# Idle PSUM banks lent to two stages in the last turns and to one in the first, with new ranks for the order of the work

## The chip, the cores and the metric

The kernel runs on one core of a Trainium2 chip. The time is the device time of one execution in microseconds (us); less is better. The core has engines that each work through a queue of their own in a fixed order: TensorE (PE) multiplies matrices and transposes, VectorE (DVE), ScalarE (ACT) and GpSimd (POOL) work element by element, and SyncE (SP) issues the DMAs of this kernel. They wait for one another through semaphores. PE writes its results to PSUM, which this kernel divides into eight tiles of 128 partitions by 512 fp32 values, here called banks; ACT and DVE read them from there.

## What is computed

The input `x` has 128 sequences of 64 tokens with 256 features (8,192 tokens), and there is one condition vector of 256 features per sequence. There are two layers, each with a residual sum:

```
x = x + ffn0(scan(cond, x))          # a gated recurrence over the 64 tokens, then an int8-quantized gated feed-forward
x = x + fp6_linear(block(x, cond))   # a hyperbolic transformer block, then a linear layer quantized to fp6
```

`block` works on vectors of a Poincare ball. It takes the log map, a layer norm, a shift and scale from the condition, and attention with 16 heads of 16 features over the 64 tokens of a sequence; then a Moebius addition of the residual; then norm, shift and scale again and a feed-forward part, which the kernel has folded into one 256 x 512 product per token (one half gives the value, the other the norm); then a second Moebius addition. `fp6_linear` scales blocks of 32 features by their largest magnitude, rounds them to a 6-bit grid, and multiplies them by a 256 x 256 weight that is rounded in the same way.

## The kernel before

The first layer's recurrence runs first, then the two products of its feed-forward part. Everything behind that, from about 373 us on, is one fused part (`fused`). It works on 64 tiles of 128 tokens, four tiles to a group (`GT` = 4), so 16 groups (`NGR`). Within a group most things are done for a pair of tiles (`h2`).

A group passes through these stages:

- `front` (matmuls at L908): the last product of the first layer, into bank `dn`;
- `norms` (L1167 on): the layer-norm coefficients, shift and scale, and the clip to the ball (L638 on DVE, L640 on POOL);
- `attention`: transposes (L95) into `qk`, ACT copies the high part (L938), DVE subtracts for the low part (L940), PE makes q, k and v (L950, `qk`), scores (L1007, `sc`), exponentials on ACT (L1016), the product with v (L1026, `ao`), ACT copies it to `raw` (L1030), DVE divides (L1033, L1034), then the output projection (L1059, `ao`) and its scaling on DVE (L1064);
- `tail`: the coefficients of the Moebius sums for a whole group (L774 to L814, with a power on POOL, L651) and the sums (L818);
- `mlp`, the feed-forward: for each pair transposes into `ml`, ACT copy (L1084) and DVE residue (L1086), then for each of the two tiles seven matmuls into `ml` (L1091, L1095), a DVE dot product (L1099) and an ACT copy (L1103) that empty the bank; after the group the scaling (L1110), the gate on POOL (L756) and square sums on ACT (L629);
- `fp6`: block maxima (L1126 to L1132), scaling on POOL (L1134), rounding on ACT (L1138), DVE dequantization (L1142), transposes into `fp`, ACT copy to the tile `yT` (L1151), products into `fp` (L1156, L1158), the residual sum on DVE (L1163), and a DMA to the output.

A loop over turns `k` from -5 to 18 staggers them. In turn `k` group `k` passes `tail`, `norms` and `mlp`, group `k + 5` passes `attention` (`LA` = 5), group `k + 6` passes `front`, and group `k - 3` passes the second half of `tail` and `fp6` (`LM` = 3). So turns -5 to -1 hold no feed-forward, no fp6 before turn 3, no `front` after turn 9, and from turn 11 there is no attention.

The turns are not run one after the other. Every operation gets a priority from its turn and from a table of ranks, and the framework's scheduler, which works while the kernel is built, puts each engine's instructions in order by these priorities and by when it expects data and buffers to be ready:

```
def step(name):
    tc.cur_priority = base + (turn_[0] + LA) * TURN + RANK[name]
```

`TURN` is 1800, so a rank of -5000 lets a stage compete with work of nearly three turns before. The order is then fixed: each engine runs its queue in that order and waits where data is late.

Banks come from pools by name. Their numbers are in `CFG`: `dn` 1, `qk` 2, `sc` 2, `ao` 1, `ml` 1, `fp` 1, eight in all. A pool with one bank makes a stage take turns with its readers: the next use may start only when the engines that read the last use have ended. The tile `yT` of fp6 has one buffer as well, and the output tile `ot` has two.

```
def bank(tag):
    return ps.tile([P, 512], F32, name=tag, tag=tag, bufs=CFG[tag])
```

Of the kernel before, what the change touches and what calls it, by code (L numbers as in the profile page):

```python
# [22 lines left out]
P = 128  # L23
# [19 lines left out]
NG = NT // GN  # L43
AR = 8
TS = 4
CFG = {'rnd': 'S', 'ef': 8, 'fill': {'x1a': 'V', 'mod0': 'V'}, 'hold': [3, 0], 'mk': 2, 'raw': 1, 'mv': 6, 'xs': 3, 'la': 3, 'sb': 7, 'qks': 'GGGG', 'deq': 'VV', 'first': 1000, 'hb': 2, 'q_h': 'P', 'q_x1': 'P', 'q_xr': 'P', 'q_ot': 'P', 'q_out': 'P', 'q_ada': 'P', 'room': [[0.3, 0.3, 0.55], [0.5, 0.4, 0.2]], 'qv': 64, 'p1': 'GVGVGVGV', 'x1': 3, 'u1': 16, 'u2': 6, 'qkv': 2, 'sq': 1, 'uT1': 2, 'uT2': 2, 'qM': 2, 'kT': 2, 'e': 4, 'oT': 1, 'yT': 1, 'hq': 2, 'hl': 2, 'xr': 1, 'ot': 2, 'ada00': 2, 'ada02': 2, 'ada10': 2, 'ada12': 4, 'dn': 1, 'qk': 2, 'sc': 2, 'ao': 1, 'ml': 1, 'fp': 1, 'mod0': 'GGGV', 'mod1': 'VVVV', 'sqm0': 'SSSS', 'sqm1': 'SSSS', 'su0': 'VVVV', 'su1': 'VGVG', 'q8': 'GGGGGG', 'hqc': 'SSSVVV', 'qm': 'SSSS', 'x1a': 'GV', 'gate0': 'GGGG', 'gate1': 'GGGG', 'yb': 'GG', 'va': 'GGGG', 'sqt': 'SSSS', 'sqg': 'SSSS', 'sqo': 'SSVS', 'f2e': 'SSSS', 'early': 0, 'q8f': 'VVVVVV', 'hqf': 'SSSVVV', 'fl': 1, 'un': 2, 'jsu': 1, 'LA': 5, 'LM': 3, 'tl': 6, 'ord': 1, 'xt': 3, 'q_xt': 'P'}
GT = 4
NGR = NTILE // GT

TURN = 1800  # L50
RANK = {"front.q8": 910, "front.cast": 539, "front.mm": -718, "front.x1": -1305, "front.add": 174, "store.x1": 0, "a.turn": -1220, "a.hi": -1577, "a.lo": 495, "a.qkv": 46, "a.qkvcopy": -917, "a.sq": 2253, "a.nh": -44, "chain.h": -8170, "a.qk": -90, "a.va": -90, "a.turnq": -90, "a.qm": -1178, "a.kt": -1474, "a.sc": -90, "a.e": -877, "a.av": -90, "a.raw": -1338, "a.o": 3284, "a.turno": 1011, "a.ot": -3468, "a.wo": 975, "a.proj": -2819, "m.turn": 987, "m.hi": -123, "m.lo": -2161, "m.mm": 1726, "m.dot": -468, "m.copy": 301, "m.a": -355, "f.max": -10889, "f.q": 4682, "f.rnd": -1889, "f.deq": 4033, "f.turn": 167, "f.yt": 4664, "f.mm": 507, "load.ot": 10015, "f.add": -588, "store.out": -58, "x2n": 2724, "own": 641, "load.xt": -636, "chain.su": 4117, "chain.full": -5861, "chain.cf": -1389, "chain.ln": -2069, "chain.tail": -2513, "stats1": 1067, "stats2": 339, "load.mod0": -1252, "load.mod1": -208, "mod0.0": -3294, "mod0.1": -93, "mod0.2": 398, "mod0.3": -712, "mod1.0": 1137, "mod1.1": 2275, "mod1.2": -5509, "mod1.3": 1054, "sqm0": 2326, "sqm1": -1277, "clip0": -1974, "clip1": -1974, "sqt0": 462, "sqt1": -162, "gate0": -1900, "gate1": 755, "sqg0": -808, "sqg1": 4262, "xdot.a": -1630, "xdot.m": 1293, "load.h": -5461, "load.x": 0, "a.sqo": 76, "load.gate0": 3865, "load.gate1": 3539, "comb.a": 708, "comb.m": -2849}

LA, LM = CFG["LA"], CFG["LM"]

# [19 lines left out]
def tile_kernel(ctx, tc, a, out):  # L74
# [70 lines left out]
    with ExitStack() as l0:  # L145
# [15 lines left out]
        with ExitStack() as sc_:  # L161
# [270 lines left out]
            for n in range(T // TS):  # L432
# [5 lines left out]
                for i in range(TS):  # L438
# [22 lines left out]
                    with tc.issue_after(lv.ins), tc.issue_after(ls.ins), tc.issue_after(lp.ins):  # L461
# [4 lines left out]
                        for q in range(2):  # L466
                            if t < CFG["hold"][q]:
                                continue
                            left[q] = [min(l, 0.0) + r for l, r in zip(left[q], CFG["room"][q])]
                            while min(left[q]) > 0:  # L470
# [25 lines left out]
        for b0 in range(0, B, NBB):  # L496
            for c in range(2):

                q8 = xp.tile([P, NBB, T], I8, name="q8", tag="q8")
                src = hsT[:, c, :, b0 : b0 + NBB].rearrange("p t b -> p b t")  # L500
                if b0 < CFG["qv"]:
                    V.tensor_scalar(q8, src, isx, None, ALU.mult)
# [16 lines left out]
        def h_chunk(pg, pu, j, at, dst):  # L519
# [3 lines left out]
            cnt[0] += 1  # L523
            if CFG["p1"][cnt[0] % 8] == "G":
                uv = fw.tile([P, GN], F32, name="uv", tag="uv")
# [34 lines left out]
        V.tensor_scalar(sdh, sd_bc, sh[:, 0:1], None, ALU.mult)  # L560

    fused(ctx, tc, a, out_tok, x_tok, locals())


def fused(ctx, tc, a, out_tok, x_tok, L):
    nc = tc.nc
    V, S, G_, PE = nc.vector, nc.scalar, nc.gpsimd, nc.tensor
# [20 lines left out]
    def move(key, out, in_):  # L588
        Q[CFG["q_" + key]].dma_start(out=out, in_=in_)

    at = [0]
    turn_ = [-LA]
    base = tc.cur_priority + 4000

    def step(name):

        tc.cur_priority = base + (turn_[0] + LA) * TURN + RANK[name]

# [13 lines left out]
    def pick(key, g):  # L612
# [3 lines left out]
            es = CFG["fill"].get(key, es)  # L616
        return es[g % len(es)]

    def bank(tag):
        return ps.tile([P, 512], F32, name=tag, tag=tag, bufs=CFG[tag])  # L620

    def big(tag, shape, dt=F32):
# [253 lines left out]
    def front(i):  # L876
# [4 lines left out]
        for h2 in pairs:  # L881
# [20 lines left out]
            move("xr", out=xr, in_=x_tok[:, i0 + 2 * h2 : i0 + 2 * h2 + 2, :])  # L902
            step("front.mm")
            py = bank("dn")

            for i, j in [(i, j) for i in range(2) for j in range(5)] + [(0, 5), (1, 5)]:
# [12 lines left out]
    def attention(i, u, sums):  # L919
# [4 lines left out]
        for h2 in pairs:  # L924
# [4 lines left out]
            uT = big("uT1", [P, 2, 2, 2 * P], F32R)  # L929
            step("a.turn")  # L930
            pt = bank("qk")
            for c in range(2):
                po = pt[:, c * 256 : (c + 1) * 256].rearrange("p (s g t) -> p s g t", s=2, g=2)
# [7 lines left out]
            for xy in range(2):  # L941
                cs = slice(xy * P, (xy + 1) * P)
                for lo, hi in ((0, 512), (512, 768)):
                    step("a.qkv")
                    pm = bank("qk")
                    n_ = hi - lo
                    PE.matmul(pm[:, :n_], lhsT=ones3[:, lo // 512, :], rhs=rows3[:, :n_], start=True, stop=False)
                    for k in range(2):
                        for q, (w, z) in enumerate(PASSES):
                            PE.matmul(pm[:, :n_], lhsT=uT[:, z, k, cs], rhs=wqkv[:, w, k, lo:hi],  # L950
                                      start=False, stop=(k == 1 and q == 2))
                    step("a.qkvcopy")
                    S.copy(qkv[:, xy, lo:hi], pm[:, :n_])
                step("a.sq")
                sq = big("sq", [P, 3 * D])
                S.activation(sq, qkv[:, xy, :], AF.Square)
                step("a.nh")
                V.tensor_reduce(nh[:, xy * 48 : (xy + 1) * 48], sq.rearrange("p (h d) -> p h d", d=HD),
                                AX.X, ALU.add)
# [342 lines left out]
```

## Time and profile before

| what | value |
|---|---|
| time, median of 3 runs | 1328.8 us (1326.1 to 1334.34) |
| profiled execution: time, span of its records | 1332.73 us, 1331.0 us |
| mean granted TensorE clock | 0.881 |
| PE busy | 1075.1 us (81%) |
| DVE busy | 1128.2 us (85%) |
| ACT busy | 847.8 us (64%) |
| POOL busy | 840.2 us (63%) |
| DVE busy between 378 and 1331 us | 842.0 of 953 us |
| last projection of the last attention (L1064) ends | 1199.7 us |

The busy shares are means over stages with different limits, so they are read stage by stage. An engine that is idle before an instruction has that idle time put down to the instruction that ended last of those it waited for. The chain of work that ended last gives DVE 6% of the span as a share of its own, PE 3%, POOL 3%, DMA 2% and ACT 1%, spread over many lines.

### The profile page before, as it was taken

The page shows a single profiled execution, that of the slowest core. Times are in us where ns is not written, and L with a number is a line of the kernel's source. Part 1 is how long each engine was busy: PE and PEld are TensorE (multiplying, and loading weights), DVE is VectorE, ACT ScalarE, POOL GpSimd, SP SyncE. Part 2 cuts the span into 40 slices and gives each one's busy share as a digit, 9 for nine tenths or more (in the row PEclk, how much of TensorE's full clock was granted, in tenths as well). Part 3 has the DMA queues.
Part 4 walks back from the last instruction along what each step waited for, and adds up shares of the span by engine and source line. Part 5 has one row for each costly group of instructions (what it writes and reads, how often), then busy time and mean ns, then how long its engine had stood idle before and what let it go on. Part 6 is the DMA issues. An engine that isn't in the chain of part 4 may idle for free. (4 is left out here: it accounts for less than half of the span.)

```text
span 1331.0 us, 23828 instructions
## 1 busy us (share of the span) xinstructions
PE 1075.1 (81%) x7382; PEld 742.9 (56%) x7404; DVE 1128.2 (85%) x3337; ACT 847.8 (64%) x2607; POOL 840.2 (63%) x1024
## 2 busy tenths in 40 slices
PE   6999977984479798988889788897888988874756
PEld 5766642332356565655666566675666756653534
DVE  5766769995787779899999999999989999799674
ACT  2455547981467677678667776776778867764331
POOL 3110118864787858878968778776686776764541
PEclk9999979995699899899899899998999869986765
DMA  7721105678843314334335245323432223323211
GB/s 240 294 70 59 54 1 201 262 276 255 259 130 106 126 33 143 113 103 146 113 124 155 89 127 159 96 69 120 135 105 80 65 72 96 96 84 91 80 43 52
DMA packets 119304, 163.64 MB, mean 123 GB/s; under 512 B 10885, under 2 KB 72074, under 8 KB 119178
## 3 DMA queue, kind: packets, MB, share of 16 engines
q1 hardware_dynamic: 119178, 162.13, 38.5%
q8 instruction: 58, 0.95, 0.3%
q14 instruction: 68, 0.56, 0.1%
HBM read 115.94 MB, written 46.14 MB: 122 GB/s over the span
## 5 line engine op out<-in xcount | busy, mean ns | idle before, releaser
L629 ACT ACTIVATE junk<-u 128x256 bf16<-128x256 f32 x432 | 182.2, 425 | 102.8 <-POOL u L756 31.4
L950 PE MATMUL qk<-wqkv,uT 128*128 128x512 f32 (+1 forms) x768 | 180.2, 374 | 10.7 <-ACT uT L938 10.5
L756 POOL TENSOR_TENSOR u<-u,ada 128x256 f32<-128x256 f32 x128 | 100.0, 785 | 86.4 <-ACT junk L629 76.3
L950 PEld LDWEIGHTS qk<-wqkv,uT 128*128 128x128 f32 x768 | 126.1, 202 | 46.5 <-issue 17.6
L1007 PE MATMUL sc<-qM,kT 64*64 64x256 f32 x1024 | 126.7, 412 | 10.9 <-ACT kT L996 9.4
L1095 PE MATMUL ml<-wm,uT 128*128 128x512 f32 (+1 forms) x384 | 122.5, 458 | 0.0
L1095 PEld LDWEIGHTS ml<-wm,uT 128*128 128x128 f32 x384 | 84.7, 223 | 51.0 <-issue 14.7
L1026 PE MATMUL ao<-va,e 128*64 128x34 f32 x2048 | 89.5, 240 | 22.0 <-DVE u L1064 13.1
L1026 PEld LDWEIGHTS ao<-va,e 128*64 128x64 f32 x2048 | 78.7, 154 | 50.1 <-DVE u L1064 16.0
L636 ACT ACTIVATE qM<-sc,mhead 128x256 f32<-128x256 f32 x256 | 102.3, 494 | 5.4 <-PE sc L95 5.4
L908 PE MATMUL dn<-wdT,hq 128*128 128x256 bf16 (+1 forms) x384 | 65.1, 310 | 38.6 <-DVE x L911 17.0
L982 POOL TENSOR_TENSOR va<-qkv,comb 64x256 f32<-64x256 f32 x128 | 87.8, 703 | 5.2 <-PE ao L1026 2.7
L629 ACT ACTIVATION_READ_ACCUMULATOR junk<-u 128x1 f32 x432 | 86.8, 201 | 0.0
L977 POOL TENSOR_TENSOR qkv<-qkv,comb 128x512 f32<-128x512 f32 x64 | 72.9, 1157 | 21.2 <-DVE comb L968 17.2
L1007 PEld LDWEIGHTS sc<-qM,kT 64*64 64x64 f32 x1024 | 56.7, 139 | 51.1 <-ACT kT L996 13.8
L445 PE MATMUL pg<-hsT,WT 128*128 128x128 f32 x504 | 76.4, 293 | 8.2 <-ACT hsT L457 7.9
L640 POOL TENSOR_SCALAR hb<-hl,cu 128x1280 int8<-128x1280 f32 (+1 forms) x64 | 64.5, 1013 | 29.1 <-DMA hl<-h_d 11.1
L1158 PE MATMUL fp<-wfT,yT 128*128 128x256 f32 x256 | 81.6, 450 | 0.0
L445 PEld LDWEIGHTS pg<-hsT,WT 128*128 128x128 f32 x504 | 66.1, 195 | 26.6 <-ACT hsT L457 23.4
L1016 ACT ACTIVATE e<-sc 128x512 f32<-128x512 f32 x128 | 74.7, 603 | 7.3 <-PE sc L1007 3.9
L527 POOL TENSOR_TENSOR hv<-uv,sil 128x512 f32<-128x512 f32 x44 | 57.9, 1318 | 29.7 <-ACT sil L521 13.0
L457 ACT ACTIVATE hsT<-gate 128x128 f32<-128x128 f32 x128 | 39.6, 309 | 53.8 <-DVE gate L456 53.8
(287 smaller groups left out, 3176.5 us busy)
## 6 DMA issues: line engine op xcount, KB each, us to landing
ada<-ada_d SPq DMA_DIRECT2D x128, 256.0 KB, 3.6
h_d<-hv SPq DMA_DIRECT2D x80, 256.0 KB, 2.2
hl<-h_d SPq DMA_DIRECT2D x32, 640.0 KB, 4.7
ada<-ada_d SPq DMA_DIRECT2D x128, 128.0 KB, 2.5
xt<-in_xT_dram SPq DMA_DIRECT2D x16, 512.0 KB, 3.7
xr<-in_x_dram SPq DMA_DIRECT2D x32, 256.0 KB, 4.1
x_d<-x SPq DMA_DIRECT2D x32, 256.0 KB, 2.9
xt<-x_d SPq DMA_DIRECT2D x32, 256.0 KB, 3.0
```

The lines of the kernel that those rows point to most:

```text
L445: lp = PE.matmul(pg[c][:, st], lhsT=WT[:, k, c * P : (c + 1) * P], rhs=hp[:, k, :], start=False, stop=False, skip_group_check=True)
L629: S.activation(junk, src, AF.Square, accum_out=acc)
L636: S.activation(dst, src, AF.Copy, scale=by)
L756: ENG[pick(f"gate{which}", g)].tensor_tensor(av, av, gb, ALU.mult)
L950: PE.matmul(pm[:, :n_], lhsT=uT[:, z, k, cs], rhs=wqkv[:, w, k, lo:hi], start=False, stop=(k == 1 and q == 2))
L977: ENG[pick("qks", g)].tensor_tensor(qk, qk, bc_in(comb[:, xy * 48 : xy * 48 + 32], HD), ALU.mult)
L982: ENG[pick("va", g)].tensor_tensor(va[r, :, s, 0:HD], qkv[r, xy, 512:768].rearrange("p (h d) -> p h d", d=HD), bc_in(comb[r, xy * 48 + 32 ...
L1007: PE.matmul(sc[rr][s * T : (s + 1) * T, c * 256 : (c + 1) * 256].rearrange("p (v t) -> p v t", v=4), lhsT=kTs[xy][r, c, s * T : (s + 1) * ...
L1016: S.activation(e.rearrange("p c v t -> p (c v t)"), sc[rr], AF.Exp, scale=1.0 / math.sqrt(HD))
L1026: PE.matmul(pv[xy * T : (xy + 1) * T, hh], lhsT=E[2 * xy + hh // 4][:, c, hh % 4, :], rhs=vas[(2 * h2 + xy) % 4][:, c * 8 + hh], start=Tru ...
L1095: PE.matmul(pm[:, cs], lhsT=uT[:, z, k, i * P : (i + 1) * P], rhs=wm[:, w, k, cs], start=False, stop=(k == 1 and q == 2))
L1158: PE.matmul(o, lhsT=yT[:, 2 * i + c, :], rhs=wfT[:, c, :], start=False, stop=(c == 1))
```

## The change

The bank of a tile is no longer fixed by its name. In turns -5 to -2 the banks of `attention` that were `ao` alternate between `ao` and `fp`. From turn 11 on the tiles of `mlp` go round `ml`, `qk`, `qk`: three tiles are taken for each pair, first the transposes, then one for each tile's products, so transposes get `ml` and products the two banks of `qk`. From turn 11 on the tiles of `fp6` alternate between `fp` and `dn`, and from turn 15 on they go round `fp`, `dn`, `ao`. Besides, 53 of the 84 ranks have new values; `CFG` has the same values, only one entry stands at another place. No operation is added or taken away, and no shape, type or engine is changed.

```
-RANK = {"front.q8": 910, ... "front.mm": -718, "front.x1": -1305, ... "a.turn": -1220, "a.hi": -1577, ... "a.qm": -1178, ... "a.proj": -2819, ... "m.hi": -123, ... "m.mm": 1726, "m.dot": -468, ... "f.add": -588, "store.out": -58, ... "chain.su": 4117, ... "chain.cf": -1389, ... "load.h": -5461, ... "comb.a": 708, ...}
+RANK = {"front.q8": 582, ... "front.mm": -1046, "front.x1": -1633, ... "a.turn": -405, "a.hi": -6857, ... "a.qm": 1669, ... "a.proj": -7498, ... "m.hi": -1065, ... "m.mm": 1399, "m.dot": -1470, ... "f.add": -4529, "store.out": 2514, ... "chain.su": 2733, ... "chain.cf": 1681, ... "load.h": -8071, ... "comb.a": 4044, ...}
...
+    used = {}
+
     def bank(tag):
+
+        k, tags = turn_[0], (tag,)
+        if tag == "ao" and k < LM - 4:
+            tags = ("ao", "fp")
+        if k >= NGR - LA:
+            tags = {"ml": ("ml", "qk", "qk"), "fp": ("fp", "dn") if k < NGR - 1 else ("fp", "dn", "ao")}.get(tag, tags)
+        n = used[tag] = used.get(tag, -1) + 1
+        tag = tags[n % len(tags)]
         return ps.tile([P, 512], F32, name=tag, tag=tag, bufs=CFG[tag])
```

More of the change, by code (lines that the diff above doesn't have):

```diff
@@ L45 @@
 TS = 4
-CFG = {'rnd': 'S', 'ef': 8, 'fill': {'x1a': 'V', 'mod0': 'V'}, 'hold': [3, 0], 'mk': 2, 'raw': 1, 'mv': 6, 'xs': 3, 'la': 3, 'sb': 7, 'qks': 'GGGG', 'deq': 'VV', 'first': 1000, 'hb': 2, 'q_h': 'P', 'q_x1': 'P', 'q_xr': 'P', 'q_ot': 'P', 'q_out': 'P', 'q_ada': 'P', 'room': [[0.3, 0.3, 0.55], [0.5, 0.4, 0.2]], 'qv': 64, 'p1': 'GVGVGVGV', 'x1': 3, 'u1': 16, 'u2': 6, 'qkv': 2, 'sq': 1, 'uT1': 2, 'uT2': 2, 'qM': 2, 'kT': 2, 'e': 4, 'oT': 1, 'yT': 1, 'hq': 2, 'hl': 2, 'xr': 1, 'ot': 2, 'ada00': 2, 'ada02': 2, 'ada10': 2, 'ada12': 4, 'dn': 1, 'qk': 2, 'sc': 2, 'ao': 1, 'ml': 1, 'fp': 1, 'mod0': 'GGGV', 'mod1': 'VVVV', 'sqm0': 'SSSS', 'sqm1': 'SSSS', 'su0': 'VVVV', 'su1': 'VGVG', 'q8': 'GGGGGG', 'hqc': 'SSSVVV', 'qm': 'SSSS', 'x1a': 'GV', 'gate0': 'GGGG', 'gate1': 'GGGG', 'yb': 'GG', 'va': 'GGGG', 'sqt': 'SSSS', 'sqg': 'SSSS', 'sqo': 'SSVS', 'f2e': 'SSSS', 'early': 0, 'q8f': 'VVVVVV', 'hqf': 'SSSVVV', 'fl': 1, 'un': 2, 'jsu': 1, 'LA': 5, 'LM': 3, 'tl': 6, 'ord': 1, 'xt': 3, 'q_xt': 'P'}
+CFG = {'rnd': 'S', 'ef': 8, 'hold': [3, 0], 'mk': 2, 'raw': 1, 'mv': 6, 'xs': 3, 'la': 3, 'sb': 7, 'qks': 'GGGG', 'deq': 'VV', 'first': 1000, 'hb': 2, 'q_h': 'P', 'q_x1': 'P', 'q_xr': 'P', 'q_ot': 'P', 'q_out': 'P', 'q_ada': 'P', 'room': [[0.3, 0.3, 0.55], [0.5, 0.4, 0.2]], 'qv': 64, 'p1': 'GVGVGVGV', 'x1': 3, 'u1': 16, 'u2': 6, 'qkv': 2, 'sq': 1, 'uT1': 2, 'uT2': 2, 'qM': 2, 'kT': 2, 'e': 4, 'oT': 1, 'yT': 1, 'hq': 2, 'hl': 2, 'xr': 1, 'ot': 2, 'ada00': 2, 'ada02': 2, 'ada10': 2, 'ada12': 4, 'dn': 1, 'qk': 2, 'sc': 2, 'ao': 1, 'ml': 1, 'fp': 1, 'mod0': 'GGGV', 'mod1': 'VVVV', 'sqm0': 'SSSS', 'sqm1': 'SSSS', 'su0': 'VVVV', 'su1': 'VGVG', 'q8': 'GGGGGG', 'hqc': 'SSSVVV', 'qm': 'SSSS', 'x1a': 'GV', 'gate0': 'GGGG', 'gate1': 'GGGG', 'yb': 'GG', 'va': 'GGGG', 'sqt': 'SSSS', 'sqg': 'SSSS', 'sqo': 'SSVS', 'f2e': 'SSSS', 'early': 0, 'q8f': 'VVVVVV', 'hqf': 'SSSVVV', 'fl': 1, 'un': 2, 'jsu': 1, 'LA': 5, 'LM': 3, 'tl': 6, 'ord': 1, 'xt': 3, 'q_xt': 'P', 'fill': {'x1a': 'V', 'mod0': 'V'}}
 GT = 4
@@ L50 @@
 TURN = 1800
-RANK = {"front.q8": 910, "front.cast": 539, "front.mm": -718, "front.x1": -1305, "front.add": 174, "store.x1": 0, "a.turn": -1220, "a.hi": -1577, "a.lo": 495, "a.qkv": 46, "a.qkvcopy": -917, "a.sq": 2253, "a.nh": -44, "chain.h": -8170, "a.qk": -90, "a.va": -90, "a.turnq": -90, "a.qm": -1178, "a.kt": -1474, "a.sc": -90, "a.e": -877, "a.av": -90, "a.raw": -1338, "a.o": 3284, "a.turno": 1011, "a.ot": -3468, "a.wo": 975, "a.proj": -2819, "m.turn": 987, "m.hi": -123, "m.lo": -2161, "m.mm": 1726, "m.dot": -468, "m.copy": 301, "m.a": -355, "f.max": -10889, "f.q": 4682, "f.rnd": -1889, "f.deq": 4033, "f.turn": 167, "f.yt": 4664, "f.mm": 507, "load.ot": 10015, "f.add": -588, "store.out": -58, "x2n": 2724, "own": 641, "load.xt": -636, "chain.su": 4117, "chain.full": -5861, "chain.cf": -1389, "chain.ln": -2069, "chain.tail": -2513, "stats1": 1067, "stats2": 339, "load.mod0": -1252, "load.mod1": -208, "mod0.0": -3294, "mod0.1": -93, "mod0.2": 398, "mod0.3": -712, "mod1.0": 1137, "mod1.1": 2275, "mod1.2": -5509, "mod1.3": 1054, "sqm0": 2326, "sqm1": -1277, "clip0": -1974, "clip1": -1974, "sqt0": 462, "sqt1": -162, "gate0": -1900, "gate1": 755, "sqg0": -808, "sqg1": 4262, "xdot.a": -1630, "xdot.m": 1293, "load.h": -5461, "load.x": 0, "a.sqo": 76, "load.gate0": 3865, "load.gate1": 3539, "comb.a": 708, "comb.m": -2849}
@@ new lines @@
+RANK = {"front.q8": 582, "front.cast": 801, "front.mm": -1046, "front.x1": -1633, "front.add": 166, "store.x1": 0, "a.turn": -405, "a.hi": -6857, "a.lo": 522, "a.qkv": 53, "a.qkvcopy": -1222, "a.sq": 2388, "a.nh": -231, "chain.h": -8170, "a.qk": -90, "a.va": -90, "a.turnq": -90, "a.qm": 1669, "a.kt": -1474, "a.sc": -90, "a.e": -31, "a.av": -90, "a.raw": -1338, "a.o": 3284, "a.turno": 1011, "a.ot": -3468, "a.wo": 975, "a.proj": -7498, "m.turn": 987, "m.hi": -1065, "m.lo": -2129, "m.mm": 1399, "m.dot": -1470, "m.copy": 301, "m.a": -410, "f.max": -10913, "f.q": 4922, "f.rnd": -1889, "f.deq": 4033, "f.turn": 167, "f.yt": 4664, "f.mm": 633, "load.ot": 9947, "f.add": -4529, "store.out": 2514, "x2n": 2132, "own": 385, "load.xt": -406, "chain.su": 2733, "chain.full": -6047, "chain.cf": 1681, "chain.ln": -2762, "chain.tail": -2988, "stats1": 1067, "stats2": -1543, "load.mod0": -1349, "load.mod1": -1335, "mod0.0": -3294, "mod0.1": -225, "mod0.2": 25, "mod0.3": -829, "mod1.0": 1309, "mod1.1": 2275, "mod1.2": -5547, "mod1.3": 1054, "sqm0": 2326, "sqm1": -1277, "clip0": -1974, "clip1": -1974, "sqt0": 368, "sqt1": 30, "gate0": -1937, "gate1": 2179, "sqg0": 523, "sqg1": 4899, "xdot.a": -1758, "xdot.m": 1090, "load.h": -8071, "load.x": 0, "a.sqo": 76, "load.gate0": 1795, "load.gate1": 3539, "comb.a": 4044, "comb.m": -2849}
```

## The prediction

> **What bounds the kernel now.** I read the busy slices first, to find which engine fills which stage. The slices of the page, 40 of 33.3 us, each digit tenths of busy time:
>
> ```profile
> PE   6999977984479798988889788897888988874756
> ...
> DVE  5766769995787779899999999999989999799674
> ...
> PEclk9999979995699899899899899998999869986765
> ```
>
> VectorE (DVE) is at nine tenths or more through most of the second half and falls only in the last five slices, where the granted TensorE clock falls too. The same by stretches, whose borders I put at the ends of single attentions (columns: window, its length, then busy time and count of PE, PEld, DVE, ACT, POOL, clock, DMA share, GB/s):
>
> ```profile
> 378.00:452.00 74.00, 63.14 (x477) 43.16 (x478) 60.45 (x130) 50.10 (x140) 61.20 (x75) 0.90 0.35 109
> 452.00:490.00 38.00, 35.59 (x301) 24.76 (x300) 26.77 (x94) 29.04 (x88) 23.41 (x26) 0.88 0.23 77
> ...
> 811.00:1118.00 307.00, 265.34 (x2162) 196.92 (x2165) 289.72 (x894) 228.21 (x749) 225.76 (x282) 0.91 0.32 97
> 1118.00:1199.00 81.00, 63.60 (x562) 48.84 (x560) 70.46 (x250) 56.40 (x202) 56.98 (x75) 0.94 0.30 94
> 1199.00:1256.00 57.00, 32.44 (x123) 24.37 (x123) 46.39 (x179) 24.52 (x87) 32.54 (x36) 0.71 0.32 97
> 1256.00:1331.00 75.00, 44.44 (x127) 30.30 (x126) 42.69 (x160) 19.89 (x67) 23.10 (x24) 0.55 0.13 42
> ```
>
> Window minus DVE busy is what better order could win: 13.6 + 11.2 us at the entry, 17.3 us in the 307 us middle, 10.6 us in 1199 to 1256 and 32.3 us in the last 75 us. The middle is DVE-bound; banks can't help there, since DVE's work is the same. The place for the new banks is the end, so I read DVE's waits from 1256 us on (us in all, times, longest):
>
> ```profile
> DVE ot L1163 <- PE fp L1158: 15.4, 5, 5.9
> DVE junk L1099 <- PE ml L1095: 5.6, 4, 2.0
> DVE satc L779 <- POOL r L651: 3.8, 2, 2.4
> ```
>
> 21 us of the 32 are waits for the two stages whose banks change. The PE timeline shows why (start, length, work, idle before it and its releaser):
>
> ```profile
> 1259.53 1.12 PE L95 MATMUL ml<-ident,u 128*128 128x128 f32 x4 [0.93 <-ACT u L1103]
> 1262.04 0.59 PE L1091 MATMUL ml<-rows,ones 128*128 128x512 bf16 x1 [1.40 <-DVE uT L1086]
> ...
> 1265.80 0.59 PE L1091 MATMUL ml<-rows,ones 128*128 128x512 bf16 x1 [0.93 <-ACT u L1103]
> ...
> 1269.56 1.11 PE L95 MATMUL ml<-ident,u 128*128 128x128 f32 x4 [0.93 <-ACT u L1103]
> ...
> 1289.58 1.03 PE L1158 MATMUL fp<-wfT,yT 128*128 128x256 f32 x4
> ...
> 1314.51 1.11 PE L95 MATMUL fp<-ident,u 128*128 128x128 f32 x4 [0.79 <-DVE ot L1163]
> ...
> 1321.13 1.12 PE L95 MATMUL fp<-ident,u 128*128 128x128 f32 x4 [0.78 <-DVE ot L1163]
> ```
>
> The last feed-forward tile pair's transpose (1259.53) waits for the copy that empties `ml`, though its input was ready at 1256.6 (L638 ends). The fp6 transpose at 1321.13 waits until DVE has added the pair before it, though its input was ready at 1311.7.
>
> **The change, part by part.**
>
> *Feed-forward, turns 11 to 15.* `ml` then serves transposes alone and the two `qk` banks take the products. From 1256.6 the last turn has two transposes (1.1 us each) and four groups of products (2.83 us each: one of L1091, six of L1095, 1262.04 to 1264.87); a group now starts 3.76 us after the one before it, the two transposes 10 us apart. New: transpose, 0.6 us copy (L1084), 0.7 us residue (L1086), so the first group starts near 1260; the four groups and the other transpose take 4 x 2.83 + 1.1 = 12.4, so the last dot (L1099) ends near 1273 where it ended at 1280.8. DVE's own work up to that dot, summed in the new order with the old rows, is 14.8 us from L638 on, so 1271.4 is its floor. The next step (L1110) has 22.1 us of DVE work from L638 before its end in both orders (1285.3 in the trace), floor 1278.7. From 1285.3 I take 5.5 us off; bounds 0 (DVE or POOL arrives no earlier) and 6.6 (the floor).
>
> *fp6, last turns.* `fp`, `dn` and, from turn 15, `ao` take turns. The last four pairs run 6.62 us apart at the end (1314.51 to 1321.13). Gone from a pair: its transpose behind the add (1.1 + 0.8 us). What stays serial is `yT`, which has one buffer (`yT`: 1): copy 0.6 and products 4.0 (1322.98 to 1326.98), with the gaps 4.7 a pair. Two pairs, from the first of the last two dequantizations (1311.0), would end near 1322.1, not 1327.7: 5.6 us. But the new DVE order puts the add of the pair before (`ot` of turn 17, L1163) in front of the last two dequantizations (L1142). That is a new wait: behind it stand both L1142, and PE's last transposes wait for them. That add needs products that now end near 1312.2 (transposes 1301.3 to 1303.5, products to 1307.5, copy, products), so dequantization ends near 1314.3 and the last add at 1325.2: gain 2.5. The products took 1.03 us a half pair at 1289.58 and 1.91 elsewhere in this stretch, where the granted clock was 1.00 and 0.50; with the second pair of turn 17 and the two behind it at the faster rate the same steps end near 1318.7, a gain of 9. I take 4, nearer the slow rows, since five of the last six pairs ran slow. The output path: loads of `ot` have two buffers and follow on SP the store of two pairs before; store and load took 2.1 + 2.6 us, so behind the add that ends near 1312.9 the last load lands near 1317.6, before its add.
>
> *Earlier drain turns.* The 2.9 us wait of L1099 for PE in 1199 to 1256 is the only other DVE wait on these banks: 1.5 us off, between 0 and 2.9.
>
> *The first turns.* Attentions 0 to 3 alternate `ao` with the idle `fp`. What PE now waits for the emptying of `ao`, from 373 to 550 us:
>
> ```profile
> PE ao L1026 <- ACT raw L1030: 0.5, 1, 0.5
> ```
>
> So the bank costs 0.5 us directly. Behind it DVE waits 6.5 us for `raw` (L1033 <- ACT raw L1030, 378 to 582), mostly latency of the attention itself. I take 1 us, between 0 and 7.
>
> *The new ranks.* 53 of 84 change, so order changes on every engine; no instruction is added or removed, on the DMA queues neither. I weigh it by work: with the old row durations summed along both built orders, when the eighth attention (7) writes its projection (L1064), DVE has done 606 us in the new order and 671 in the old. That looks like a delay of feed-forward, but compare at equal DVE work: in the old order DVE had done 607 us when attention 6 ended, and there PE had 289 us of work behind it and ACT 514; the new order has 293 and 521 at its 606. The engines are as balanced as before; at 514 and 566 us PE and ACT are 12 to 19 us further ahead than before, which is the risk. At the end L638 of the last turn has 1093.9 us of DVE work in front of it, against 1093.4. So I put the ranks at 0, bounds -21 (half of the 42 us of idle of entry and middle) and +32 (below).
>
> *Sum.* 5.5 + 4 + 1.5 + 1 = 12 us. The profiled execution took 1332.7 us for a span of 1331.0, so 1320.7 for its like. It lay 3.9 us over the median of the three runs, 1328.8; from that median the forecast is 1316.8, **1317 us**.
>
> **A rule weighed against it.** The one warm half pair at 1289.58 came after 5 us of nearly unbroken matmuls (1281.57 to 1287.3). The Trainium skill, TensorE: Matmul & The Clock Gate, section "A second HAM failure mode: psum-queue depth-cycling", speaks against a change like this: cycling through banks with short pauses between groups made the clock swing between half and full, and the throughput suffered. By that rule the last products stay slow and the fp6 term is 2.5, the sum 10.5; the same page's Part 1, where some 3.4 us of sustained work frees the clock, would make it 9, the sum 17. No row of this trace shows either with these banks.
>
> **Rivals.**
>
> *Slower: attention runs ahead and DVE starves.* One mechanism, at 450 to 750 us: with less feed-forward work in front of attention 7, DVE has 65 us less filler (671 - 606) while attention's own chain (raw, exponentials, square sums) keeps its length. Against: equal balance above; for: entry stretches, where attention ran with little filler, idle 11.2 of 38 us. If half of the 65 us is lost the run ends at 1317 + 32 = 1349. It decides from 12 us of added idle: attention 7 would have to end later than about 763 us (751 + 12).
>
> *The banks are hidden.* DVE and POOL order, not PE, ends the drain: POOL's power (L651, 2.9 us each) and the ACT/POOL ping-pong of the gates stay. Then only the fp6 lower bound of 2.5 and the earlier turns' 1.5 remain: 4 us, 1325.
>
> *More than forecast.* Denser PE gets its clock in the last 75 us (9 instead of 4, 6.6 instead of 5.5) and the ranks win some 12 of those 42 us: 1317 - 18 = 1299.
>
> *It doesn't do what it says.* The product tile could land on the bank that it waits for anyway; but in the built order the last turns' products sit on `qk` and their transposes on `ml`, so I give this nothing of its own.
>
> **How the numbers follow.** Forecast (1308 to 1323) 0.44, of which 0.22 below 1315.5; more 0.20; hidden (1323 to 1334) 0.16; starving 0.20, of which 0.17 over 1342. This measurement can tell about 1% (13 us) from no change. Faster 0.22 + 0.20 = 0.42; slower 0.17; the same 0.22 + 0.16 + 0.03 = 0.41. The range leaves out the worst of the starving case (0.14) and the best of "more" (0.05): 1298 to 1340.
>
> **What would show it.** L1163's wait for PE after 1256 falls from 15.4 to under 10 us; L1099's falls below 3; the last two fp6 adds stand under 5 us apart where they stood 6.6; PE clock in the last 75 us over 0.55. DVE idle from 378 to 811 stays near 40 us; if it passes 55, the ranks cost what the banks won. The forecast is wrong if L638 of the last turn comes much later or earlier than the same work in front of it says, or if attention 7 ends after 763 us.

## The result: less time at the end, more in the middle

The changed kernel took 1334.43 us in the median of 20 runs (1327.44 to 1341.1), the kernel before 1327.21 us (1320.03 to 1334.34, also 20). The ratio is 1.0051 with a 95% interval of 1.0032 to 1.0071: some 7 us slower, where 12 us faster was forecast. The profiled execution of the changed kernel took 1335.15 us for a span of 1333.4, against 1332.73 and 1331.0 before. So the profile of before lies 5.5 us over its kernel's median and that of the changed kernel 0.7 us, and differences between the two profiles have to be read with that in mind.

Line numbers from L626 on are higher by 10 in the changed kernel (L638 becomes L648, L1163 becomes L1173). The busy slices of its page:

```profile
PE   6999976984579898999887798879989789983754
...
DVE  5766779996687779897898977999979989889876
...
PEclk9999979995589899798987898979989799767978
```

The DVE row shows both halves of the story. The last five slices are fuller in all (89876 where 99674 stood), and the middle has sevens and eights where it had nines. The granted TensorE clock of the last two slices is 7 and 8 where it was 6 and 5.

Windows that end at single attentions say how much. The stretch from the end of attention 3 (its last L1064 or L1074) to the end of attention 13 holds 513 us of DVE work by the old row durations in both kernels. First the kernel before (window, length, then busy time of PE, PEld, DVE, ACT, POOL, clock, DMA share, GB/s):

```profile
582.00:1118.00 536.00, 461.13 (x3715) 341.20 (x3717) 511.65 (x1571) 395.47 (x1290) 408.37 (x497) 0.92 0.36 107
```

and the changed kernel, in its middle and in its last stretch:

```profile
563.00:1125.00 562.00, 487.61 (x3722) 357.79 (x3724) 506.27 (x1559) 399.67 (x1291) 413.94 (x506) 0.89 0.35 106
```

```profile
1266.00:1333.00 67.00, 35.00 (x133) 24.86 (x132) 47.35 (x176) 23.05 (x80) 29.78 (x30) 0.79 0.20 62
```

The same work takes 562 us instead of 536, and DVE is idle for 562 - 506.3 = 55.7 us of it, where it was idle for 24.4. In the last 67 us it is idle for 19.7, where it was for 32.3 in the last 75.

The waits of DVE from 1256 us on answer to those shown of before:

```profile
DVE satc L789 <- POOL r L661: 7.3, 3, 4.6
DVE ot L1173 <- PE dn L1168: 3.1, 1, 3.1
DVE ot L1173 <- PE fp L1168: 2.1, 1, 2.1
...
DVE ot L1173 <- PE ao L1168: 0.6, 1, 0.6
```

The residual add of fp6 waits 5.8 us for PE in all, where it waited 15.4, and the wait of the feed-forward's dot product (5.6 us before) is not in the answer any more. In its place POOL's power (L661) has come forward. On PE the last two turns of fp6 now look like this:

```profile
1314.20 1.08 PE L95 MATMUL dn<-ident,u 128*128 128x128 f32 x4
...
1315.29 1.91 PE L1168 MATMUL fp<-wfT,yT 128*128 128x256 f32 x4
...
1319.52 1.13 PE L1168 MATMUL ao<-wfT,yT 128*128 128x256 f32 x4 [0.73 <-ACT yT L1161]
...
1323.70 0.63 PE L95 MATMUL ao<-ident,u 128*128 128x128 f32 x4
...
1325.54 1.03 PE L1168 MATMUL dn<-wfT,yT 128*128 128x256 f32 x4
```

The second pair's transpose runs beside the first pair's work without a wait, half a pair's products take 1.03 us instead of 1.91 from the second pair on, and the one gap left inside a turn is that for the single tile `yT` (0.73 us).

From the last L638 (L648) to the last residual add, both with as good as the same DVE work in front of them (1093.4 and 1093.9 us), it took 1256.6 to 1327.7 = 71.1 us before and 1276.6 to 1330.1 = 53.5 us after: 17.6 us less. Not all of that is due to the banks: the granted clock differed too, and the run with fp6's banks alone (below) shows that it does so without any change. But that L648 ended 20.0 us later. Where these 20 us arose is seen by subtracting, at the end of single attentions, the DVE work in front (old row durations, summed along the built order) from the time. (That sum comes to 1141 us in all, where DVE was busy for 1128.2 us, so the remainder is somewhat less than DVE's idle time, in all kernels alike. Its differences are what counts.)

| end of attention | 3 | 7 | 8 | 11 | 13 | 15 | last L638/L648 |
|---|---|---|---|---|---|---|---|
| before: time - DVE work, us | 133.5 | 140.7 | 147.5 | 154.4 | 156.2 | 160.7 | 163.2 |
| after | 131.5 | 151.4 | 168.4 | 175.0 | 179.8 | 181.8 | 182.7 |

Up to attention 3, in the turns with the lent bank, nothing is lost. From there to attention 8 the changed kernel loses 23 us (36.9 us of added idle against 14.0), and behind it no more.

What ended DVE's idle time in that middle, before (582 to 1118 us; the answer's largest groups):

```profile
DVE tftc L786 <- ACT zztc L785: 4.3, 4, 2.6
DVE u L739 <- DMA ada<-ada_d: 3.9, 3, 2.6
DVE lnaln L710 <- POOL lnaln L651: 3.8, 4, 1.5
```

and after (563 to 1125 us):

```profile
DVE nh L968 <- ACT sq L966: 6.0, 5, 2.2
DVE uT L950 <- ACT uT L948: 4.8, 3, 2.4
DVE u L749 <- DMA ada<-ada_d: 4.2, 6, 0.9
DVE q L784 <- ACT junk L639: 4.1, 1, 4.1
DVE rden L1043 <- ACT raw L1040: 3.9, 4, 1.4
```

All groups of the two answers summed: 29 waits of 19.6 us before, of which ACT ended 6.8 and PE 0.9; 54 waits of 51.1 us after, of which ACT ended 30.0 and PE 6.4. No single wait stands out. DVE meets, at many places, an instruction whose input is not finished, most often by ACT, and everything behind it in DVE's queue stands still, for 0.9 us in the mean and 4.1 us at most. Three of these instructions belong to attention itself (L968, L950 and L1043): they waited 14.7 us for ACT, where the same three waited 0.6 us before.

### The profile page after: what moved, and what is told of

The parts are those of the page before. It is cut to its first block, busy times and chain, and to the rows that moved or that the text cites. A ratio compares the mean times of both kernels' runs of the same rounds, so it can differ in the third digit from the quotient of the medians.

```text
span 1333.4 us, 23814 instructions
## 1 busy us (share of the span) xinstructions
PE 1092.0 (82%) x7378; PEld 753.7 (57%) x7404; DVE 1117.2 (84%) x3337; ACT 849.4 (64%) x2607; POOL 835.2 (63%) x1024
## 4 chain that ended last, share of the span: by engine, by line
DVE 44%; PE 23%; POOL 11%; ACT 8%; DMA 7%; issue 5%; SPq 0%; POOLq 0%; DVEq 0%; ACTq 0%
PE pg L445 5%; DMA ada<-ada_d 5%; DVE u L828 4%; PE pg L426 3%; DVE u L749 3%; DVE am L530 2%; DVE nh L968 2%; PE sc L1017 2%; PE qk L960 2%; DVE junk L774 2%; DVE hv L529 2%; ACT qM L646 2%; DVE bn L726 2%; POOL r L661 2%; DVE u L648 2%
## 5 line engine op out<-in xcount | busy, mean ns | idle before, releaser
L960 PEld LDWEIGHTS qk<-wqkv,uT 128*128 128x128 f32 x768 | 125.6, 202 | 48.4 <-issue 24.4
L1017 PE MATMUL sc<-qM,kT 64*64 64x256 f32 x1024 | 135.9, 437 | 15.1 <-ACT kT L1006 8.9
L918 PE MATMUL dn<-wdT,hq 128*128 128x256 bf16 (+1 forms) x384 | 69.3, 328 | 38.6 <-DVE x L921 17.7
L1017 PEld LDWEIGHTS sc<-qM,kT 64*64 64x64 f32 x1024 | 59.7, 147 | 59.3 <-issue 17.3
L992 POOL TENSOR_TENSOR va<-qkv,comb 64x256 f32<-64x256 f32 x128 | 84.2, 677 | 10.5 <-PE ao L1036 6.0
L987 POOL TENSOR_TENSOR qkv<-qkv,comb 128x512 f32<-128x512 f32 x64 | 70.6, 1111 | 20.6 <-DVE comb L978 10.0
L1105 PE MATMUL ml<-wm,uT 128*128 128x384 f32 (+1 forms) x264 | 76.7, 424 | 0.0
L968 DVE TENSOR_REDUCE nh<-sq 128x48 f32<-128x768 f32 x64 | 60.1, 939 | 19.4 <-ACT sq L966 19.2
L918 PEld LDWEIGHTS <-hq 128*128 128x128 bf16 (+1 forms) x384 | 38.9, 113 | 65.6 <-ACT junk L639 20.5
```

Source lines behind the costliest of these rows:

```text
L918: PE.matmul(py[:, i * D : (i + 1) * D], lhsT=hq[r, j, i * P : (i + 1) * P], rhs=wdT[r, j, :], start=(i == 0 and j == 0), stop=(j == 5), sk ...
L992: ENG[pick("va", g)].tensor_tensor(va[r, :, s, 0:HD], qkv[r, xy, 512:768].rearrange("p (h d) -> p h d", d=HD), bc_in(comb[r, xy * 48 + 32 ...
L1017: PE.matmul(sc[rr][s * T : (s + 1) * T, c * 256 : (c + 1) * 256].rearrange("p (v t) -> p v t", v=4), lhsT=kTs[xy][r, c, s * T : (s + 1) * ...
L1105: PE.matmul(pm[:, cs], lhsT=uT[:, z, k, i * P : (i + 1) * P], rhs=wm[:, w, k, cs], start=False, stop=(k == 1 and q == 2))
```

## The experiments

Three theories went into the first four kernels. A: the new ranks cost the middle. B: the bank lent in the first turns costs it. C: the end only looks shorter because work was moved out of it.

**The banks of the last turns alone.**

```
-RANK = {new values}
+RANK = {values of before}
...
-        if tag == "ao" and k < LM - 4:
-            tags = ("ao", "fp")
```

> Only the lending of banks from turn 11 on, with the old ranks and no lending in the first turns. Each engine's order is that of the kernel before up to 847 us of DVE work, about 1000 us into the span. In the changed kernel the stretch from the last turn's L638 to the last add shrank from 71 to about 54 us. Theory A (new ranks cost the middle, end banks win the end): 15 to 18 us faster, ratio 0.986 to 0.989. Theory B (the bank lent in the first turns costs the middle): the same ratio, 0.986 to 0.989. Theory C (the end only looks shorter because other work was moved out of it): ratio 0.995 to 1.000.

Measured: ratio 1.0002 (0.9976 to 1.0029). None of the theories had the overall time. The profile again shows a shorter end: from the last L638 to the last add 1274.4 to 1325.2 = 50.8 us, against 71.1, with 4.7 us more DVE work in front of that L638 (1098.1 us against 1093.4). But time less DVE work, which followed the kernel before within 2 to 5 us as far as attention 12 (160.8 against 156.8), had grown to 169.1 at attention 13, 177.4 at 14 and 176.3 at L638, against 156.2, 164.8 and 163.2. The order changed at 847 us of DVE work, about 1000 us into the span, when the new banks changed what the scheduler found ready. So what the end gained was lost again just before it.

**The banks of the last turns with the new ranks, without the one in the first turns.**

```
-        if tag == "ao" and k < LM - 4:
-            tags = ("ao", "fp")
```

> The lending from turn 11 on with the new ranks, without the bank lent to attention in the first turns. Theory A (new ranks cost some 22 us before the end): about as the changed kernel, ratio 1.003 to 1.007. Theory B (the first turns' bank costs it): 15 us faster than before, ratio 0.986 to 0.992.

Measured: 1.0229 (1.019 to 1.0269), far over what either theory gave. Time less DVE work was 155.4 us at attention 7, 181.8 at 11 and 195.9 at 15.

**All lent banks with the old ranks.**

```
-RANK = {new values}
+RANK = {values of before}
```

> All banks lent as in the changed kernel, old ranks. Attention 7 ends with 629 us of DVE work in front of it (671 before, 606 in the changed kernel). Theory A: the loss goes with the ranks, ratio 0.985 to 0.990. Theory B: the loss stays, ratio 1.002 to 1.008.

Measured: 1.0268 (1.0222 to 1.0314). The loss did not go with the ranks as A had it, nor did it stay as B had it: it grew.

**The new ranks alone.**

```
-RANK = {values of before}
+RANK = {new values}
```

(as a change of the kernel before; every tile keeps its bank)

> The new ranks alone, every tile in its old bank. Attention 7 ends with 644 us of DVE work in front of it. Theory A: the loss in the middle stays and the gain at the end is gone, ratio 1.013 to 1.020. Theory B: no loss and no gain, ratio 0.998 to 1.003.

Measured: 1.026 (1.0221 to 1.0298). Each half of the change, the ranks or the banks, costs more than two per cent by itself, and so do the new ranks with the banks of the last turns alone (1.0229); only the banks of the last turns with the old ranks, which leave the order alone for the first 1000 us, cost nothing. That led to theory D: the old order fits the old banks on this chip, and leaving it for any other order costs DVE some two per cent.

**Only fp6's banks, only from turn 16 on**, so that the order before stays as it was:

```
+        if tag == "fp" and k >= 16:
+            tags = ("fp", "dn", "ao")
```

(old ranks, nothing else lent)

> Old ranks; only fp6 rotates over fp, dn and ao, and only from turn 16 on. The order on every engine is that of the kernel before up to 1120 us of DVE work of 1141 (VectorE's row 3261 of 3323), so nothing but the banks differs until the last 40 us. Theory A' (lent banks do win the end where the order is left alone): the last two turns' pairs no longer wait for the residual add, 4 to 9 us faster, ratio 0.993 to 0.997. Theory C (the end's gain comes from the moved work): ratio 0.999 to 1.001.

Measured: 0.9963 (0.9938 to 0.9989), 5 us faster, as A' had it. C falls: the order is the old one as far as 1120 us of DVE work, so nothing was moved out of the end. In its profile the end of the last dequantization (1313.1) and the last add (1320.7) stand 7.6 us apart, where they stood 16.0 apart before (two residual adds lie between, where three did). The waits of the add:

```profile
DVE ot L1171 <- PE dn L1166: 4.1, 1, 4.1
...
DVE ot L1171 <- PE fp L1166: 2.1, 1, 2.1
DVE ot L1171 <- PE ao L1166: 0.8, 1, 0.8
```

7.0 us, where they were 15.4.

This run shows one thing more. From the last L638 to the end of the last dot product of the feed-forward (L1099, here L1107) it has the order and the banks of before; nothing is lent there. The windows, first of before, then of this run:

```profile
1256.60:1280.80 24.20, 15.53 (x42) 11.00 (x40) 15.61 (x69) 8.35 (x32) 10.42 (x11) 0.50 0.07 22
```

```profile
1262.50:1282.80 20.30, 9.73 (x41) 6.93 (x39) 16.28 (x70) 8.29 (x32) 10.59 (x11) 0.92 0.08 27
```

The same work stood at a granted clock of 0.92 instead of 0.50, took 3.9 us less, and the dot product waited 1.5 us for PE instead of 5.6. Two executions differ that much in a stretch where nothing was changed. So a shorter end between two single profiles is no measure of what the banks win; the times of all runs are (here some 5 us).

**The feed-forward's banks from turn 11 and fp6's from turn 16.**

```
+        if tag == "ml" and k >= 11:
+            tags = ("ml", "qk", "qk")
+        if tag == "fp" and k >= 16:
+            tags = ("fp", "dn", "ao")
```

(old ranks)

> Old ranks; the feed-forward's products go to the two qk banks from turn 11, fp6 rotates from turn 16. The order is the old one up to 980 us of DVE work (about 1140 us into the span). Theory A': up to 18 us of gain behind the last turn's L638 as in the run with all end banks (24.5 us of DVE idle there before, 6.1 in that run), less what the new order costs between 980 us of work and there: ratio 0.988 to 0.996. Theory D (any other order than the tuned one loses as much as the banks win): ratio 0.998 to 1.002.

Measured: 0.997 (0.9948 to 0.9992), at the edge between the two: no better than fp6's banks alone. Here the order leaves the old one at 980 us of DVE work. So what the feed-forward's banks win in that order can't be told from what the order costs.

**The changed kernel without the banks at the end.**

```
-        if k >= NGR - LA:
-            tags = {"ml": ("ml", "qk", "qk"), "fp": ("fp", "dn") if k < NGR - 1 else ("fp", "dn", "ao")}.get(tag, tags)
```

> The changed kernel without the banks lent at the end: new ranks, ao alternating with fp in the first turns. Attention 7 has 606 us of DVE work in front of it and attention 11 has 846, as in the changed kernel. The changed kernel's DVE idle was 21 us more than the old one's when its last attention ended. Theory A': the changed kernel's gain at the end is missing: 15 to 18 us slower than it, ratio to the kernel before 1.016 to 1.020. If the end banks win nothing: ratio 1.003 to 1.007.

Measured: 1.0164 (1.0126 to 1.0203), against 1.0051 with these banks. The difference, 0.0113 or 15 us (9 to 21 us with the two intervals combined), is what the banks at the end are worth under the new ranks, as A' expected, together with what they change in the order behind 1120 us, where the two kernels' orders part. The two profiles are 20.6 us apart: 8.2 us in front of the last L638 (1284.8 us here, 1276.6 in the changed kernel) and the rest behind it. Time less DVE work goes as in the changed kernel: 152.7 us at attention 7, 168.7 at 8, 178.6 at 11. The transposes wait for the add again:

```profile
1324.81 1.12 PE L95 MATMUL fp<-ident,u 128*128 128x128 f32 x4 [0.79 <-DVE ot L1171]
...
1346.58 0.66 PE L95 MATMUL fp<-ident,u 128*128 128x128 f32 x4 [0.79 <-DVE ot L1171]
```

The last two adds also show what the clock does without any lent bank:

```profile
1345.83 0.69 DVE L1171 TENSOR_TENSOR ot<-fp,ot 128x512 f32<-128x512 f32 x1 [4.94 <-PE fp L1166]
1350.11 0.69 DVE L1171 TENSOR_TENSOR ot<-fp,ot 128x512 f32<-128x512 f32 x1 [3.59 <-PE fp L1166]
```

They stand 4.3 us apart, with half pairs of products at 1.03 us. In the profile of before, where these half pairs took 1.91 us, they stood 6.6 us apart; in the changed kernel, with three banks and 1.03 us, 2.8 us.

**A control: the kernel before with ranks moved at random**, each by +150 or -150.

> The kernel before, every rank moved by +150 or -150 at random (a twelfth of a turn); no bank is lent. Attention 7 has 647 us of DVE work in front of it. Theory D (the order before is fitted to its banks, and any departure loses some two per cent, as the three mixed runs did with 1.023 to 1.027): ratio 1.010 to 1.030. Against it, that the loss belongs to the particular new ranks or to the first turns' bank: ratio 0.998 to 1.005.

Measured: 1.0198 (1.0162 to 1.0234). A change with no purpose at all, and no bank lent, costs 2%.

A second draw:

> A second draw of +150 or -150 on every rank, no bank lent; it says how far the cost of an untuned order scatters. Theory D: ratio 1.010 to 1.030, as the first draw (1.020).

Measured: 1.0253 (1.0211 to 1.0296).

A third, with only +40 or -40:

> The kernel before with every rank moved by +40 or -40 at random (a forty-fifth of a turn), no bank lent. Theory D: the loss comes from leaving the tuned order at all, so even this costs 1 to 2.5 per cent, ratio 1.010 to 1.025. If small moves are harmless and only wide ones cost: ratio 0.998 to 1.005.

Measured: 1.028 (1.0247 to 1.0313); a smaller move cost no less. In this last run the window from 582 to 1150 us holds, at 568 us of length, 515.4 us of busy DVE, so 52.6 us of idle, and its waits are of the same many kinds:

```profile
DVE u L739 <- DMA ada<-ada_d: 8.6, 7, 2.4
DVE ot L1163 <- PE fp L1158: 7.2, 3, 3.2
DVE tftc L786 <- ACT zztc L785: 3.9, 4, 1.8
DVE rden L1033 <- ACT raw L1030: 3.2, 3, 2.0
```

In the three draws attention 7 ended with 633 to 647 us of DVE work in front of it (606 in the changed kernel), and time less DVE work was 157.8 to 161.5 us there (151.4 in the changed kernel, 140.7 before). So the loss doesn't follow how far attention runs ahead. But it did run ahead in every run that lost time in the middle (606 to 647 us, against 671 in the kernel before and in the runs that kept its order that far), so no run here separates the two.

**The feed-forward's banks from turn 14 alone, fp6's from turn 16** (old ranks; the edit is that of the run with turn 11, with 14 in its place).

> Old ranks; the feed-forward's products go to the qk banks from turn 14 alone, fp6 rotates from turn 16. The old order holds up to 980 us of DVE work, and attentions 14 and 15 end with 998 and 1039 us in front of them, as before (997 and 1039). If the end banks win 15 us wherever the order before them is as good as the old: ratio 0.987 to 0.993, better than the run with fp6 alone (0.9963). If the new order behind 980 us costs its share again: 0.995 to 0.999.

Measured: 0.9989 (0.9967 to 1.0012). The order again leaves the old one at 980 us of DVE work, and the run is not faster than before. Attention 15 ended as before (161.3 us of time less DVE work, against 160.7), but the last L638 came at 1277.2 us instead of 1256.6, with 1109.5 us of DVE work in front of it instead of 1093.4. Other work was put ahead of the feed-forward of the last turn.

**fp6's banks from turn 16, and two tiles for the transposed copy** in those turns (the attention's `oT`, idle by then, serves the second pair):

```
...
-            yT = big("yT", [P, 4, P])
+            yT = big("oT" if turn_[0] >= 16 and h2 % 2 else "yT", [P, 4, P])
```

> As the run with fp6 rotating from turn 16, and there the second pair's transposed copy goes into the attention's idle tile of the same shape, so that the two pairs no longer share the single yT. In that run the second pair's products waited 0.7 us for the copy in each of the three turns: up to 2 us faster than it, ratio 0.994 to 0.997.

Measured: 0.9956 (0.9933 to 0.9979). On PE the second pair's products follow the first pair's without the gap of 0.7 us:

```profile
1311.81 1.03 PE L1166 MATMUL dn<-wfT,yT 128*128 128x256 f32 x4
1312.68 1.03 PE L1166 MATMUL fp<-wfT,oT 128*128 128x256 f32 x4
```

That 0.0007 can't be told from the run without it, but the kernel is faster than the one before and, by ratios of 0.9956 and 1.0051, than the changed one.

## Why the prediction was wrong

*What bounds the kernel* held: DVE in the middle, latency at the end, and the waits of L1099 and L1163 for PE there.

*Feed-forward at the end*: the step from the last L638 to the end of L1110 was forecast 5.5 us shorter, at most 6.6. It went from 28.7 to 21.4 us, 7.3 shorter, as the work in front of it passed in somewhat less than the 22.1 us of the old rows. The banks did what was forecast, since no wait of the dot product for PE is left. But the size is not theirs alone: with fp6's banks only, where the feed-forward kept its one bank, the step took 24.8 us at a faster clock.

*fp6 at the end*: forecast 4 us, with 9 if the products ran at the faster clock. From the end of the last dequantization to the last add it went from 16.0 to 6.6 us, and from L1110 to that dequantization from 26.4 to 25.5: 10.3 us together. The faster clock came, and the new wait (the add in front of the last dequantizations) cost DVE 0.65 us. The term was sized from the slow rows of one execution, and such rows are not the rule: in the five runs with no bank lent at the end and another order (the new ranks alone, those with the first turns' bank, and the three draws) the last two adds stand 4.3 us apart, not 6.6. Of the 3.8 us between 6.6 and the 2.8 of the changed kernel, 2.3 are there without these banks and 1.5 come with them. By the times of the runs, fp6's banks in the old order win some 5 us, close to the 4 us of the term. The term lay near the slow rows, which other executions did not have, so that it comes out near is in part luck.

The rule that was weighed against the change, of the Trainium skill, TensorE: Matmul & The Clock Gate, section "A second HAM failure mode: psum-queue depth-cycling", did not show itself here: the granted clock of the last 67 us was 0.79 with the lent banks, where it was 0.55 in the last 75 without; as the clock also differs by itself, that is no proof against the rule. The page's Part 1 agrees with one stretch: in the run with fp6's banks from turn 16 PE began dense work at 1302.97, and its first fast row stands at 1306.18, 3.2 us later, where the page gives some 3.4. Other stretches don't show it: in the profile of before PE worked from 1307.88 to the end with no gap over 0.8 us, and every row was slow.

*The first turns*: forecast 1 us. Time less DVE work at attention 3 was 131.5 against 133.5, within what one profile scatters. What the lent bank costs or wins behind that is part of the new order.

*The new ranks* were the step that failed: the cost of the new order, which it put at 0 because at equal DVE work PE and ACT had as much work in front of them as before (293 and 521 us against 289 and 514). Those sums were right, and they say nothing about stalls. A queue that is executed in its built order stops at an instruction whose input comes late, however well the totals are balanced. DVE stopped 54 times instead of 29, for 51.1 us instead of 19.6. The bounds of the step (-21 to +32) held the 20 us that it cost; the value taken in them did not. One of the prediction's own signs said so: DVE was idle for 62.9 us from 378 to 811 us, where it was for 40.2 before and 55 was the mark for ranks that cost what the banks won.

The step also asked whether the *new* order is good, and not how good the *old* one is. The three random draws answer that: a move of every rank by 40 or by 150, against turns of 1800, costs 2 to 3%. By its idle time the changed kernel lies close to these (182.7 us of time less DVE work at the last L638, the draws 188.9 to 199.3, the kernel before 163.2). The new ranks are not bad in themselves. With all banks lent they are faster than the old ranks (1.0051 against 1.0268), and under them the bank of the first turns is a gain (1.0051 with it, 1.0229 without). A reading that fits all this, though no run tests it further, is that each set of ranks fits its own banks, and that the old pair has the better order.

*The rivals*: the slower one had its place nearly right (450 to 750 us; the loss fell at 600 to 850) and its point of decision wrong. Attention 7 ended at 757.7 us, before the 763 from which it was to decide, and 17 us of idle time came right behind it. Its mechanism, DVE without filler because attention runs ahead, is neither shown nor excluded. The draws lose as much with less running ahead, but 14.7 of the 51.1 us of waits in the middle are those of attention's own three instructions for ACT. That the banks would be hidden was wrong: they were worth some 15 us under the new ranks.

Together: in the profiles 17.6 us less behind the last L638 and 20.0 us more before it, and some 7 us slower over the 20 runs. The two agree if some 5 of the 17.6 us are the slow clock at the end of the one profile of before, which lay 5.5 us over its median; that is an estimate, and no run shows it directly. What the runs leave open is which part of the middle's loss belongs to the ranks and which to the bank of the first turns: every one of these edits builds a new order, and no run lent that bank with the old order kept. Nor was the old order kept with the feed-forward's banks lent.

## What to carry to other kernels

Where the order on the queues is rebuilt from the buffers, as here, a change of buffers has two effects: what the buffer wins where it is used, and what the rebuilt order costs or wins everywhere behind the point where it first differs. Find that point before forecasting, and where it lies early, weigh the cost of any new order by a control with ranks moved at random; sums of work per engine don't show it. A lent buffer can be kept cheap by lending it only where the order no longer has time to go astray, as the banks from turn 16 on were here. And before an end stretch is called won, the same stretch of other runs shows how much of it comes and goes with the clock.

## What the runs showed of the hardware

The granted clock at the end is not a property of the kernel alone. In the last feed-forward, with the same order and the same banks, it was 0.50 in the profile of before and 0.92 in that with fp6's banks from turn 16, and a half pair of fp6 products takes 1.91 us at the slow clock and 1.03 at the fast one. What decides between the two no run here shows: in the last 16.0 us to the last add of before PE was busy for 12.25 us (77%) at 0.50, while in the run with the new ranks and the first turns' bank it was busy for 6.99 of the last 9.9 us (71%) at 0.77.

Two executions with the same order scatter by several microseconds in the middle: at the end of attention 15, with 1039.0 us of DVE work in front of it, the profiles of the kernel before and of the two with fp6's banks from turn 16 stood at 1199.7, 1206.1 and 1200.4 us. A difference of 5 us between two single profiles says little.
